# Graph attention on 200,000 edges: twelve chunks of the second superchunk gathered as rows of x, and the first superchunk's edge work placed between its row products

## The chip, the cores and the metric

The kernel runs on one core of a Trainium2 chip. The metric is the device time of one execution in microseconds (us); lower is better. A kernel's time is the median of several executions.

## The reference

A graph with 6250 nodes of 256 features and 200,000 edges, sorted by destination, goes through a layer norm, a ReLU and two graph-attention layers (four heads of 64, then one head of 256), with residuals around them. Cut to what matters:

```python
h = relu(layernorm(x))                      # 6250 x 256
# each layer, on its own input x (h, then the first layer's output):
te = relu(edge_attr @ We + be) * exp(x @ Wo + bo)[src][:, None]   # one row per edge
src2, dst2, ea2 = add_self_loops(src, dst, te, n)   # a loop's attributes: the mean of its node's edges
hx = (x @ Wg).reshape(n, heads, f)
al = leaky_relu(hx.a_s[src2] + hx.a_d[dst2] + (ea2 @ Wge).a_e, 0.2)
m  = segment_max(al, dst2)
al = exp(al - m[dst2]);  al = al / segment_sum(al, dst2)[dst2]
out = segment_sum(hx[src2] * al, dst2) + b
# layer 0: x = relu(out + x)      layer 1: x = out + x, and the first input is added
```

Every edge needs the projected row `hx[src]` of its source node, its logit, the maximum over the edges of its destination, and a weighted sum per destination.

## The kernel before, in words

Edges lie in chunks of 128 (one edge to a partition), and up to C = 24 chunks make a superchunk: 66 superchunks in each layer, 132 steps in all. The instructions of each engine are issued in the order in which they are written; nothing reorders them.

**The prologue** (`prologue`, from L221) makes layer 0's table T, in DRAM: for each node the projected row, its attention terms and the layer-norm pair. The nodes lie in NT = 49 tiles of 128. For a tile, DVE takes the statistics (`stats`, L287), with the Newton steps of the reciprocal root on POOL for the middle groups (L310 to L324); ACT normalises (`norm`, L336); PE transposes twice (`turn`, L342) into a PSUM tile `pT` and ACT copies that back (L344); PE multiplies by the weights in two matmuls, which the trace shows as four (`mult` and `node_rows`, L481) into one of five PSUM tiles `ps`; DVE adds the bias and stores the row in SBUF (`keep` and `node_store`, L485). Tiles go in groups of up to GT = 7; `store` writes a group's rows to T by one DMA from SyncE (L361). Three row tiles `trow` are used in turn.

The 24 chunks of superchunk 0 don't wait for the table: `first_rows` (L276) has POOL gather the rows of x themselves into the gather tile G0, and after the 49 table tiles 24 more row products, through the same five steps, turn them into table rows in place. One loop (L386) is software-pipelined over all 73 tiles; its counter is k, and f = k - NT counts the products after the tables. Between its products the loop calls the other generators: the folds of the attention vectors into the weights (`fold`, L184 to L201, and `fold_e`, L204 to L217; at f = 4, 7 and 12), and one step of the index work per iteration (`indices` and `index_group`, DVE, small operations) once the tables are past. The gathers of x rows are paced by

```python
if k < 9 or k >= 14 and k % 2:
    next(rows0, None)
```

**The edge loop** (`edges`, L693) starts when the prologue is over and its SBUF and PSUM pools are closed. It opens its own: the gather tiles of the second and third superchunk, one-hots, work tiles and three PSUM pools. It then does superchunk 0's first half: `spread` and `parts` (DVE L1113, PE L1228), `blocks`, `rphase1` (PE L1089, ACT L1090), `rphase2` (PE L1098), `adst` (PE L1242), `onehots` (DVE L1207) and `edge_rows` (DVE L1256). Each turn k of the loop does the second half of step k and the first half of step k+1: `gather` of a later step, `logits` (DVE), `ends` (PE L1294), `links` (DVE L1304, L1306, PE L1311), `maxima`, the weighting of the gathered rows (`scale` on DVE, L1378, in layer 0; `scale_rows` on ACT, L1387, in layer 1), `carried` (L1360 to L1368), and the `sums`: 24 matmuls of one-hot by weighted rows (PE L1397), evicted by ACT (L1402).

**Gathers** (`gather`, L989) are POOL's indirect DMAs, one per chunk, from the table. There are three G tiles. The rows of step k+3 go into the tile of step k, each chunk once the sums have read it (`own` in the loop, L746); before the change steps 1 and 2 are gathered in full (24 chunks each) as soon as the table is written, and step 0 not at all, since its rows come from the prologue:

```python
for c in range(0) if st["k"] == 0 and self.CX > last else range(last + 1) if own else (last, *range(last)):
    nc.gpsimd.indirect_dma_start(...)
```

Of the kernel before, what the change touches and what calls it, by code (L numbers as in the profile page):

```python
# [24 lines left out]
I32 = mybir.dt.int32  # L25
# [56 lines left out]
class Kernel:  # L82
# [10 lines left out]
    def run(self):  # L93
# [9 lines left out]
        with ExitStack() as c:  # L103
# [7 lines left out]
            self.prologue()  # L111
# [4 lines left out]
    def consts(self, wp):  # L116
# [104 lines left out]
    def prologue(self):  # L221
# [4 lines left out]
        GT = 7  # L226
        CX = self.CX = min(self.cs[0], NX)
        V = nc.vector
        with ExitStack() as c:
            xp = self.pool("x", 1, c)  # L230
            trows = [xp.tile([P, GT, L.TW], F32, name=f"trow{i}") for i in range(3)]
            wp = self.pool("pw", 2, c)
            pt = self.pool("pt", 2, c, space=PSUM)
# [14 lines left out]
            src0 = wp.tile([P, CX], I32, name="src0", bufs=1)  # L248
            nc.sync.dma_start(src0, a["src"][:, 0:CX])
            load(1)  # L250
            fold, fold_e, edge_weights, more = self.consts(wp)
# [16 lines left out]
            zero = wp.tile([P, L.TW], F32, name="zero", bufs=1)  # L268
            nc.gpsimd.memset(zero, 0.0)
            if NT * P < N + P:  # L270
                nc.sync.dma_start(self.T[0][NT * P:N + P, :], zero[:N + P - NT * P, :L.TW])
            ln = wp.tile([P, NT + CX, 2], F32, name="ln", bufs=1)

            self.G0 = G0 = self.gp[0].tile([P, C, 270], F32, name="G")

            def first_rows():  # L276
# [10 lines left out]
            def stats(*gs):  # L287
# [3 lines left out]
                st = wp.tile([P, w, 6], F32, name=f"st{w}", bufs=2)  # L291
# [45 lines left out]

            def turn(g, i, t):
                pT = pt.tile([P, 2, P], F32, name="pT")
# [6 lines left out]
            def mult(g, i, t):  # L346
                pss[t] = pt.tile([P, 512], F32, name="ps", bufs=5)
                self.node_rows(L, hTs.pop(t), pss[t])

            def keep(g, i, t):  # L350
                row = G0[:, t - NT, :] if g >= g0 else trows[g % 3][:, i, :]
                self.node_store(L, pss.pop(t), row)
                if g >= g0 and i == len(groups[g]) - 1:
                    v = G0[:, t - NT - i:t - NT + 1, L.g:L.g + 1]
                    nc.scalar.activation(v, v, AF.Exp)

            def store(g):
                n, ts, trow = len(groups[g]), groups[g], trows[g % 3]
                nc.scalar.activation(trow[:, :n, L.ln:L.ln + 2], ln[:, ts[0]:ts[0] + n, :], AF.Copy)
                nc.scalar.activation(trow[:, :n, L.g:L.g + 1], trow[:, :n, L.g:L.g + 1], AF.Exp)  # L360
                nc.sync.dma_start(self.T[0][0:NT * P, :].rearrange("(p t) d -> p t d", p=P)[:, ts[0]:ts[0] + n, :],  # L361
# [22 lines left out]
            index = self.indices(wp)  # L384
            kept = 0
            for k in range(-3, len(tiles) + 1):  # L386
                if k == 28:
                    next(index)
                    gi = self.index_load(0, wp)
                    index = chain(index, self.index_group(0, wp, gi))  # L390
                if k > NT + 1:
                    next(index, None)
# [4 lines left out]
                if k == 31:  # L397
                    none = a["x"][N:N + 2 * P, :].rearrange("n d -> (n d)")
# [1369 lines left out]
```

## Time and profile before

| | |
|---|---|
| three runs, us | 4916.92, 4930.53, 4933.85; median 4930.53 |
| the profiled execution, us | 4941.52; its span 4939.7 |
| mean granted TensorE clock | 0.723 |
| PE busy | 2933.2 us, 59% of the span |
| DVE busy | 2452.5 us, 50% |
| ACT busy | 1123.3 us, 23% |
| POOL busy | 2998.2 us, 61% |
| DMA | 592.01 MB, mean 120 GB/s |

The profile is of one execution. Busy time is the time in which an engine executes; PE's weight loads are counted apart (PEld) and overlap with its matmuls. A row of the timeline gives the start (us from the start of the span), the busy time, the engine, line and operation with its operands (out<-in), the number of instructions put together in the row, and in brackets the idle time before it and what ended it; "issue" means that nothing the profile shows was waited for. A group in the table of costliest groups gives busy us, mean ns of one, and idle time before.

### The profile page before, as it was taken

How to read it: one execution, taken by the hardware profiler on the slowest of the kernel's cores; microseconds unless marked ns; L12 is line 12 of the kernel's file. 1: busy time of each engine (PE TensorE's matmuls, PEld its weight loads, DVE VectorE, ACT ScalarE, POOL GpSimd, SP SyncE). 2: the span in 40 equal slices, each digit the busy share in tenths (PEclk: the TensorE clock that was granted, in tenths of full speed). 3: DMA queues.
4: the chain of work that ended last, by engine and by line, in shares of the span. 5: the costliest groups of instructions: out<-in, count | busy, mean ns of one | idle time of the engine just before them, and what ended most of it. 6: DMA issues, size and time to landing. Idle time of an engine off the chain costs nothing.

```text
span 4939.7 us, 37929 instructions
## 1 busy us (share of the span) xinstructions
PE 2933.2 (59%) x10028; PEld 1839.7 (37%) x10028; DVE 2452.5 (50%) x6092; ACT 1123.3 (23%) x2676; POOL 2998.2 (61%) x3217
## 2 busy tenths in 40 slices
PE   7455666666666666666555555656556565655656
PEld 5233333434334343434333333333333333333334
DVE  5366666667666666666644333333333333333335
ACT  4111111111111111111102333323333332333322
POOL 5346666666666666666644666666666666666663
PEclk8677777777777777777777666666666666666667
DMA  6234444444444444444433444444444444443442
GB/s 196 79 98 126 126 135 123 135 129 135 124 129 135 128 128 130 135 121 131 129 109 91 115 114 111 118 112 114 119 113 114 114 120 113 112 120 106 117 118 70
DMA packets 248198, 592.01 MB, mean 120 GB/s; under 512 B 65827, under 2 KB 105209, under 8 KB 247739
## 3 DMA queue, kind: packets, MB, share of 16 engines
q0 software_dynamic: 150048, 422.59, 32.8%
q1 hardware_dynamic: 96957, 164.82, 10.3%
q10 hardware_dynamic: 976, 2.12, 0.1%
q8 instruction: 86, 1.41, 0.1%
q14 instruction: 131, 1.07, 0.1%
HBM read 544.19 MB, written 45.36 MB: 119 GB/s over the span
## 4 chain that ended last, share of the span: by engine, by line
issue 30%; PE 29%; DVE 22%; POOL 10%; another core or an unknown queue 5%; DMA 3%; ACT 1%; DVEq 0%; ACTq 0%
PE u L1397 21%; POOL G L989 10%; DVE G L1378 8%; DMA G<-T,src 3%; PE y L1089 3%; DVE S L1207 2%; PE zad L1098 2%; PE ps L481 1%; DVE m L1326 1%; DVE rt L1256 1%; DVE lb L1113 1%; ACT R L1090 1%; DVE fa L1472 1%; DVE t1row L1562 0%
## 5 line engine op out<-in xcount | busy, mean ns | idle before, releaser
L989 POOL DMA_INDIRECT G<-T,src x3078 | 2934.8, 953 | 1826.8 <-issue 943.2
L1397 PE MATMUL u<-G,S 128*128 128x270 f32 (+1 forms) x6232 | 1873.1, 448 | 1416.3 <-issue 1167.5
L1397 PEld LDWEIGHTS u<-G,S 128*128 128x128 f32 x6232 | 1361.9, 221 | 1860.8 <-issue 1376.8
L1387 ACT ACTIVATE G<-G,kw 128x256 f32<-128x256 f32 x1512 | 609.0, 496 | 0.0
L1304 DVE TENSOR_TENSOR_SCAN cl<-fl,cl,lf 4x129 f32<-4x129 f32 (+1 forms) x130 | 61.1, 470 | 1037.9 <-PE zad L1228 945.9
L1402 ACT ACTIVATE U<-u 128x270 f32<-128x270 f32 (+1 forms) x131 | 51.6, 394 | 2203.3 <-PE u L1397 1642.8
L1378 DVE TENSOR_TENSOR G<-G,kps 128x6144 f32<-128x6144 f32 (+4 forms) x83 | 441.3, 5331 | 0.0
L1207 DVE TENSOR_TENSOR S<-kps,loc 128x3072 f32<-128x3072 f32 x132 | 437.7, 3316 | 4.6
L1089 PE MATMUL y<-ea,webd 64*128 64x256 f32 (+2 forms) x1056 | 358.3, 770 | 45.3 <-ACT R L1090 37.7
L1098 PE MATMUL zad<-R,wea 128*64 128x384 f32 (+1 forms) x1056 | 288.2, 684 | 156.9 <-ACT R L1090 79.1
L1090 ACT ACTIVATE R<-y,webd 128x1024 f32<-128x1024 f32 (+3 forms) x264 | 235.6, 892 | 441.3 <-issue 177.7
L1098 PEld LDWEIGHTS zad<-R,wea 128*64 128x64 f32 x1056 | 83.2, 177 | 395.9 <-issue 247.2
L1429 DVE SCALAR_TENSOR_TENSOR mg<-U,mw 128x1 f32<-128x1 f32 x66 | 14.7, 223 | 347.7 <-ACT mw L1427 176.7
L1089 PEld LDWEIGHTS y<-ea,webd 64*128 64x128 f32 x1056 | 117.0, 271 | 110.6 <-issue 60.4
L1256 DVE STREAM_TRANSPOSE rt<-zad 128x768 f32<-128x768 f32 (+1 forms) x130 | 125.8, 968 | 5.1 <-PE zad L1242 5.1
L481 PE MATMUL ps<-wg,hT 128*128 128x266 f32 x292 | 91.3, 441 | 54.5 <-issue 35.2
L481 PE MATMUL fin<-wg,h1T 128*128 128x260 f32 x264 | 117.1, 588 | 1.6 <-ACT h1T L1489 1.6
L1113 DVE TENSOR_TENSOR lb<-lb,kps 128x1536 bf16<-128x1536 bf16 (+1 forms) x68 | 113.0, 1662 | 0.0
L1360 DVE SCALAR_TENSOR_TENSOR G<-U,kw,G 1x257 f32<-1x257 f32 x62 | 29.5, 475 | 155.9 <-issue 93.1
L1499 ACT ACTIVATE t1row<-t1row 128x1 f32<-128x1 f32 x66 | 13.4, 203 | 368.6 <-DVE t1row L485 160.6
L1311 PE MATMUL lf<-ident,cl 36*128 36x36 f32 (+1 forms) x132 | 37.7, 286 | 94.4 <-issue 60.5
L1294 PE MATMUL lf<-ident,fb 128*36 128x128 f32 (+1 forms) x132 | 52.3, 396 | 57.8 <-DVE fb L1287 45.6
(241 smaller groups left out, 2273.5 us busy)
## 6 DMA issues: line engine op xcount, KB each, us to landing
G<-T,src POOLq DMA_INDIRECT x3078
ea<-in_ea_dram SPq DMA_DIRECT2D x64, 768.0 KB
lb<-locrow SPq DMA_DIRECT2D x64, 384.0 KB
nd<-t1row SPq DMA_DIRECT2D x66, 225.8 KB
tw<-nd SPq DMA_DIRECT2D x66, 225.8 KB
tw<-T SPq DMA_DIRECT2D x66, 117.2 KB
T<-t1row SPq DMA_DIRECT2D x66, 113.8 KB
tw<-in_x_dram SPq DMA_DIRECT2D x66, 112.0 KB
```

The source lines that it names most:

```text
L481: self.nc.tensor.matmul(ps[:, :L.MW], hT[:, k, :], self.wg[L.l][:, k, :], start=(k == 0), stop=(k == 1))
L989: nc.gpsimd.indirect_dma_start(out=G[:, c, 0:L.TW], out_offset=None, in_=st.get("from", self.T[L.l])[0:self.N, :], in_offset=bass.Indirect ...
L1089: nc.tensor.matmul(y[:, i, :n], self.webd[l][r, :], ea[r, w], start=True, stop=True)
L1090: nc.scalar.activation(R[:, :, w], y[:, :, :n], AF.Relu, bias=self.be[l])
L1098: nc.tensor.matmul(st["zad"][i * PH:(i + 1) * PH, o], self.wea[l][0], R[:, i, w], start=True, stop=False)
L1113: V.tensor_tensor(lb[:, :, :n], lb[:, :, :n], self.k_part.unsqueeze(2).to_broadcast([P, i, n]), op=OP.is_equal)
L1207: nc.vector.tensor_tensor(st["S"][:, c0:c1, :], self.k_iota.unsqueeze(1).to_broadcast(w), self.loc[:, o + c0:o + c1].unsqueeze(2).to_broad ...
L1256: V.transpose(rv[:, :32 * c].rearrange("p (b n) -> p b n", b=2), z.rearrange("p (b n) -> p b n", b=2)[:, :, :16 * c])
L1304: V.tensor_tensor_scan(cl[:H, :], fl[:H, :], lf[:H, 0:P + 1], init, op0=OP.add, op1=OP.max)
L1378: nc.vector.tensor_tensor(v, v, pw[:, c0:c1, :].unsqueeze(3) .to_broadcast([P, c1 - c0, H, L.F]), op=OP.mult)
L1387: self.nc.scalar.activation(v, v, AF.Copy, scale=st["w"][:, c:c + 1])
L1397: nc.tensor.matmul(st["u"][:, :L.W], S[:, i, :], G[:, i, 0:L.W], start=(j == 0), stop=(j == c - 1))
```

## The change

**Gathers.** `first_rows` goes on after superchunk 0's 24 chunks and gathers the rows of x of the first CX1 = 12 chunks of superchunk 1, into a one-hot tile that is not yet needed (X). Twelve more tiles join the prologue's loop: 36 row products follow the tables instead of 24, f runs to 35, and the last twelve write into superchunk 1's G tile. `gather` of step 1 then issues 12 gathers from the table instead of 24. The pace of the x gathers changes from every second iteration to every iteration from k = 34 on.

**Pools.** The one-hot, work and index pools are opened at the start. The prologue's x, row and PSUM pools (`early`) are closed at f = 0, right after the last table store; the edge loop's gather and PSUM pools are opened there (`edge_pools`), and the gathers of step 1 (and, as before, of step 2) follow. From then on the row products alternate between two PSUM banks, and the transposes have one, all borrowed from the edge loop's pools (`Banks`, `turned_bank`, `row_bank`). Some scratch tiles share memory with tiles that are used later.

**Table stores.** Rows are stored in groups of GS = 5 tiles (ten stores) rather than in the groups of the loads.

**Order.** `first_edges` runs superchunk 0's edge work between the row products, each piece at a given f, up to the `sums`, whose 24 matmuls go in four pieces at f = 29, 31, 33 and 35. The edge loop leaves out for k = 0 what is done. Index steps start before the tables end (eight in k = 38 to 45) and then go two to an iteration. Folds move from f = 4, 7, 12 to f = 4, 16, 20.

```diff
@@ run
+            self.sp, self.wp, self.xp = (self.pool(n, b, c, side="right") for n, b in (("onehot", 2), ("work", 2), ("index", 1)))
@@ prologue
-        GT = 7
+        GT, GS = 7, 5
         CX = self.CX = min(self.cs[0], NX)
+        CX1 = self.CX1 = min(NX // 2, self.cs[1] - 1) if self.NS > 12 else 0
+        early = ExitStack()
         with ExitStack() as c:
-            xp = self.pool("x", 1, c)
-            trows = [xp.tile([P, GT, L.TW], F32, name=f"trow{i}") for i in range(3)]
-            wp = self.pool("pw", 2, c)
-            pt = self.pool("pt", 2, c, space=PSUM)
+            wp = self.pool("pw", 2, c, side="right")
+            xp = self.pool("x", 1, early)
+            pt = self.pool("pt", 2, early, space=PSUM)
+            trows = [xp.tile([P, GS, L.TW], F32, name=f"trow{i}") for i in range(3)]
...
+            X = self.sp.tile([P, C, P], F32, name="S").rearrange("p (c k) d -> p c (k d)", k=2)
             def first_rows():
...
+                for i in range(CX1):
+                    nc.gpsimd.indirect_dma_start(
+                        out=X[:, i, :], out_offset=None, in_=a["x"][0:N, :],
+                        in_offset=bass.IndirectOffsetOnAxis(ap=src0[:, CX + i:CX + i + 1], axis=0))
+                    yield
...
+            if CX1:
+                xs[len(groups)] = X
+                groups.append(list(range(NT + CX, NT + CX + CX1)))
...
+            def turned_bank(t=0):
+                if t < NT + CX:
+                    q = self.ps_1.tile([P, 512], F32, name="u")[:, 0:2 * P]
+                else:
+                    q = self.ps_1.tile([P, 1024], F32, name="zad")[:, 0:2 * P]
+                return q.rearrange("p (k n) -> p k n", k=2)
+            def row_bank(t=0):
+                banks[0] += 1
+                if banks[0] % 2:
+                    return self.ps_f.tile([P, 512], F32, name="fin")
+                if t < NT + CX:
+                    return self.ps_1.tile([P, 512], F32, name="lf")
+                return self.ps_y.tile([P, 2, 512], F32, name="y")[:, 0, :]
...
-                pT = pt.tile([P, 2, P], F32, name="pT")
+                pT = pt.tile([P, 2, P], F32, name="pT") if t <= NT else turned_bank(t)
...
-                pss[t] = pt.tile([P, 512], F32, name="ps", bufs=5)
+                pss[t] = pt.tile([P, 512], F32, name="ps", bufs=5) if t < NT else row_bank(t)
...
                 if f == 0:
                     keep(*tiles[k - 1])
-                    while kept < g0:
+                    while kept < stores:
                         store(kept)
                         kept += 1
                     self.load_ea(0)
+                    drain(rows0)
+                    early.close()
+                    self.edge_pools(ctx)
+                    self.gather(s0)
+                    self.gather(s1)
+                    pt = Banks()
+                if f in (4, 16, 20):
+                    folds.append(fold(self.L[1], pt) if f == 16 else fold_e(self.L[f // 20], pt))
+                    next(folds[0])
...
-                if k >= NT - 1:
-                    step(g + 2)
+                if NT - 1 <= k < NT:
                     step(g + 2)
                 step(g + 2)
-                if t >= NT:
-                    step(g + 2)
-                if k < 9 or k >= 14 and k % 2:
+                if NT - 11 <= k < NT - 3:
+                    next(index, None)
+                if f >= 0:
+                    next(index, None)
+                    next(index, None)
+                if k < 9 or 14 <= k < 34 and k % 2 or k >= 34:
                     next(rows0, None)
-                if f == 12:
+                if f == 4:
+                    self.nodes(s0)
+                if f == 6:
...
+                self.first_edges(s0, f)
...
+            for q in range(len(tiles) + 1 - NT, 37):
+                self.first_edges(s0, q)
+        self.np_ = self.pool("nodes", 2, ctx, side="right", reuse_waits="tile")
+
+    def first_edges(self, st, f):
+        if f == 11:
+            st["y"] = self.rphase1(st)
+            next(st["y"])
+        if f == 12:
+            self.spread(st)
+            self.parts(st)
+        if f == 14:
+            self.blocks(st)
+            drain(st["y"])
+            self.load_ea(1)
+        if f == 16:
+            self.rphase2(st)
+            self.adst(st)
+        if f == 18:
+            self.edge_rows(st)
+        if 15 <= f < 23 and f % 2:
+            self.onehots(st, 3 * (f - 15), 3 * (f - 13))
+        if f == 24:
+            self.lf = self.ps_1.tile([P, 512], F32, name="lf")
+            self.nc.vector.memset(self.lf[0:4, 0:1], -BIG)
+            drain(self.logits(st))
+        if f == 25:
+            self.ends(st)
+        if f == 26:
+            self.links(st)
+        if f == 27:
+            drain(self.maxima(st))
+        if 28 <= f < 36 and f % 2 == 0:
+            drain(self.scale(st, cuts=(3 * (f - 28), 3 * (f - 26))))
+        if 29 <= f < 37 and f % 2:
+            self.sums(st, (3 * (f - 29), 3 * (f - 27)))
...
+    def edge_pools(self, ctx):
+        self.gp += [self.pool(f"gath{i}", 1, ctx, reuse_waits="tile") for i in range(1, 3)]
+        self.ps_y, self.ps_1, self.ps_f = (self.pool(n, 1, ctx, space=PSUM, reuse_waits="tile") for n in ("ps_y", "ps_1", "ps_f"))
+        self.state = {0: None, 1: None}
...
@@ edges, the loop
-            self.gather(nx)
-            st["rows"] = st["L"].l
-            drain(self.logits(st))
-            self.ends(st)
+            if k:
+                self.gather(nx)
+                st["rows"] = st["L"].l
+                drain(self.logits(st))
+                self.ends(st)
...
@@ gather
-        for c in range(0) if st["k"] == 0 and self.CX > last else range(last + 1) if own else (last, *range(last)):
+        c0 = (self.CX, self.CX1, 0)[min(st["k"], 2)]
+        for c in range(last + 1) if own else (last, *range(c0, last)) if c0 <= last else ():
```

More of the change, by code (lines that the diff above doesn't have):

```diff
@@ L382, in step @@
                         del ahead[q]
-            index = self.indices(wp)
-            kept = 0
+            s0, s1 = self.steps[:2]
+            index = self.indices(wp, drow)
+            kept, stores = 0, -(-NT // GS)
             for k in range(-3, len(tiles) + 1):
+                f = k - NT
                 if k == 28:
                     next(index)
[L389 to L392, printed above, removed]
+                    gi = self.index_load(0, self.xp)
+                    index = chain(index, self.index_group(0, self.xp, gi))
                 if k == 1:
@@ L492, in indices @@
         V = nc.vector
-        sc0 = wp.tile([P, 11, NS], I32, name="sc0", bufs=1)
+        n = 11 * NS
+        t = self.trows1.rearrange("p i w -> p (i w)")
+        assert 2 * n <= t.shape[1] and C * P >= 4 * 32 * C
+        sc0, scf = (x.rearrange("p (k s) -> p k s", s=NS) for x in (t[:, 0:n].bitcast(I32), t[:, n:2 * n]))
         nc.sync.dma_start(sc0, a["sdst"].partition_broadcast(P))
@@ L766, in edges @@
                 self.onehots(st)
-            if st["rows"]:
-                self.scale_rows(st)
-            else:
-                drain(self.scale(st))
-            self.carried(st)
-            self.sums(st)
+            if k:
+                if st["rows"]:
+                    self.scale_rows(st)
+                else:
+                    drain(self.scale(st))
+                self.carried(st)
+                self.sums(st)
             if late:
```

109 lines of the change are left out of this document (47 added, 62 removed).

## The prediction

> **What bounds the kernel now.** I read the page first, for the whole span and its costliest engine.
>
> ```profile
> span 4939.7 us, 37929 instructions
> L989 POOL DMA_INDIRECT G<-T,src x3078 | 2934.8, 953 | 1826.8 <-issue 943.2
> ```
>
> POOL issues 3078 gathers of table rows and is otherwise idle for 1826.8 us, so neither POOL nor any other engine fills the span. 132 superchunks (66 in each of two layers) share the 4939.7 us: 37.4 us each. The change edits only the start, up to the sums of superchunk 0; the loop behind is instruction for instruction as before and hangs on one chain: the gather of superchunk k+3 refills the G tile that the sums of superchunk k free. So the whole span should move by what the start of superchunk 1's sums moves by. That start is the quantity I work out.
>
> Next the timeline of POOL, for the gather runs of the start.
>
> ```profile
> 91.92 1.07 POOL L989 DMA_INDIRECT G<-T,src  x1 [14.90 <-ACT hT L344]
> ...
> 151.58 0.95 POOL L989 DMA_INDIRECT G<-T,src  x1 [0.30 <-issue]
> 210.17 0.95 POOL L989 DMA_INDIRECT G<-T,src  x1 [57.64 <-issue]
> ...
> 238.99 0.95 POOL L989 DMA_INDIRECT G<-T,src  x1 [0.30 <-issue]
> ```
>
> The first run is 48 gathers, those of superchunks 1 and 2, from 91.92 to 152.53, 1.27 us apart (59.66 us over 47 steps). The second, of superchunk 3, waits 57.64 us for the sums of superchunk 0 and ends at 239.94. Now the timeline of PE in the same stretch, and the windows view (length, then busy us and count of PE, PEld, DVE, ACT, POOL, then granted clock, DMA share, GB/s):
>
> ```profile
> 123.68 2.14 PE L481 MATMUL ps<-wg,hT 128*128 128x266 f32 x4 [11.17 <-issue]
> 157.69 2.14 PE L481 MATMUL ps<-wg,hT 128*128 128x266 f32 x4 [12.77 <-ACT hT L344]
> 208.68 11.21 PE L1397 MATMUL u<-G,S 128*128 128x270 f32 x48 [0.95 <-DVE G L1378]
> 242.24 0.32 PE L1311 MATMUL lf<-ident,cl 36*128 36x36 f32 x1 [21.23 <-DVE cl L1306]
> 253.95 11.21 PE L1397 MATMUL u<-G,S 128*128 128x270 f32 x48 [2.16 <-DVE G L1368]
> ```
> ```profile
> 91.90:112.60 20.70, 11.74 (x45) 9.02 (x43) 7.84 (x39) 4.35 (x11) 15.80 (x17) 0.75 0.43 119
> 112.60:157.20 44.60, 5.13 (x12) 3.27 (x12) 1.53 (x5) 1.74 (x4) 30.48 (x32) 0.54 0.41 111
> 219.90:241.20 21.30, 0.91 (x6) 0.40 (x5) 0.20 (x2) 0.57 (x2) 15.17 (x16) 0.62 0.42 109
> 254.90:267.80 12.90, 11.42 (x54) 8.88 (x52) 10.84 (x35) 1.16 (x3) 9.85 (x10) 1.00 0.48 118
> 267.80:287.30 19.50, 0.00 (x0) 0.00 (x0) 0.15 (x1) 0.84 (x3) 13.27 (x14) 0.54 0.42 115
> 300.20:315.20 15.00, 12.96 (x53) 9.99 (x51) 12.67 (x34) 1.12 (x3) 11.36 (x12) 0.89 0.54 148
> 357.50:381.00 23.50, 17.05 (x70) 11.51 (x68) 19.47 (x41) 3.96 (x10) 18.01 (x19) 0.93 0.61 174
> 381.00:390.00 9.00, 1.57 (x3) 0.84 (x4) 0.85 (x6) 0.00 (x0) 4.99 (x6) 0.75 0.46 126
> ```
>
> This is what sets the start. From the first gather of a run PE gets through 45, 54, 53 or 70 matmuls and then nearly stops, with DVE and ACT, until POOL's run ends: 12 matmuls in 44.6 us, 6 in 21.3, none in 19.5, 3 in 9.0. POOL keeps its pace throughout. The profile doesn't say why; I use it as a rule of this kernel, "some 50 matmuls per gather run". Superchunk 0's last row products and all its edge work lie between these stalls, and superchunk 1's sums start at 253.95.
>
> **The change, part by part.** f counts row products after the 49 table tiles. Before, f ends at 23; now it ends at 35.
>
> *Twelve gathers moved ahead.* They leave the first run (48 becomes 36) and join the gathers of x rows, on POOL's queue. There they stand in front of POOL's last block of layer-norm statistics:
>
> ```profile
> 68.45 0.25 POOL L324 TENSOR_SCALAR ln<-sc 128x7 f32<-128x7 f32 x1
> 72.64 0.21 POOL L312 TENSOR_TENSOR sc<-sc 128x13 f32<-128x13 f32 x1 [3.94 <-DVE sc L306]
> ...
> 76.76 0.26 POOL L324 TENSOR_SCALAR ln<-sc 128x13 f32<-128x13 f32 x1
> 77.06 0.60 ACT L336 ACTIVATE h<-x,ln 128x256 f32<-128x256 f32 x1 [1.05 <-POOL ln L324]
> ```
>
> ACT already waits for that block, so there is no slack. By the order of the step calls the block is issued in iteration 37; the new gathers of iterations 27, 29, 31, 33, 34, 35 and 36 precede it. Seven at 1.27 us from 68.70 end at 77.6, the block of 4.38 us at 82.0, not 77.0: 5.0 us late, and tables and first run with it. The tables' last store now holds four tiles, not two: 0 to 2 us, 1 taken. The run starts at 91.9+6.0 = 97.9 and its 36 gathers end at 97.9+45.7 = 143.6. PE came back 5.2 us after the first run (157.69) and 2.3 after the second (242.24); with 3.7, at 147.3.
>
> *How far PE is by then.* Before, it had row product f=10 ahead of it at 157.69; within the run it also folded layer 1's node weights (12 matmuls), which the change puts off. A product is 6 matmuls, two transposes included, so the same allowance reaches f=12.
>
> *From there to the sums.* These rows give the pace:
>
> ```profile
> 162.54 0.64 PE L184 MATMUL pT<-ident,wge 128*128 128x128 f32 x2
> 164.58 0.67 PE L342 MATMUL pT<-ident,h 128*128 128x128 f32 x2
> 165.04 1.98 PE L481 MATMUL ps<-wg,hT 128*128 128x266 f32 x4
> 167.24 1.98 PE L481 MATMUL ps<-wg,hT 128*128 128x266 f32 x4
> 172.15 1.06 PE L481 MATMUL ps<-wg,hT 128*128 128x266 f32 x4
> 173.27 1.06 PE L481 MATMUL ps<-wg,hT 128*128 128x266 f32 x4
> 185.63 0.17 PE L1228 MATMUL zad<-a,Q 128*128 128x12 bf16 x1 [4.80 <-DVE a L1223]
> 185.73 1.23 PE L1089 MATMUL y<-ea,webd 64*128 64x256 f32 x4
> 187.79 2.08 PE L1089 MATMUL y<-ea,webd 64*128 64x512 f32 x4 [0.84 <-ACT R L1090]
> 191.08 2.83 PE L1098 MATMUL zad<-R,wea 128*64 128x384 f32 x8 [1.22 <-ACT R L1090]
> 193.84 0.69 PE L1242 MATMUL zad<-lb,aq 128*128 128x384 bf16 x2
> ```
>
> Sums of superchunk 0 begin at f=29. Seventeen products: three at the 2.20 us seen after a stall, fourteen at 1.12, 22.3. Superchunk 0's own PE work, now between them: 1.23+2.08+2.83+0.69 = 6.8. Folds: the edge one took 2.04 (162.54 to 164.58), the node one has twice the transposes, 6.1 together. PE waiting in line for DVE is new: the edge pieces stand in PE's queue between two products, and the next product, with ACT and the row store behind it, waits. The longest is
>
> ```profile
> 182.78 1.78 DVE L1113 TENSOR_TENSOR lb<-lb,kps 128x1536 bf16<-128x1536 bf16 x1
> ```
>
> and its followers, until the 185.63 above: 2.85. With the waits for logits and links, and two PSUM banks for products where there were five, I take 7 (none at best; 14 if no piece is hidden). In all 42.2: the sums begin at 189.5, not 208.68. Index and one-hot work on DVE costs nothing beside PE as long as DVE keeps up; if not, see the third rival.
>
> *The tail.* The gathers of superchunk 3 start 1.5 us after the sums, at 191.0, and the rule applies again: from f=29 PE has 8 products and 24 sums, 96 matmuls. With 58 done it would stop; 18 gathers are free by then and end at 213.9; 2.3 us later PE runs the other 38 in 8.0: 224.2. Without a stop 8x1.12+11.21 = 20.2 suffice: 209.7. But here POOL in turn pauses whenever PE is late, which no run of before shows, so I take the middle, 217.0. Then superchunk 1 needs, undisturbed, what superchunk 0 needed from 185.63 to 208.68, 23.1: its sums start at 240.1, against 253.95. **Gain 14 us.**
>
> The profiled execution took 4941.52 us, 1.8 more than its span; the three timed runs are 4916.92 to 4933.85, median 4930.53, 11 below it. 4941.5-14 = 4927.5 on the profile's scale, 4916.5 on the median's. A change under 0.3% (14.8 us) can't be told from none here.
>
> [...] First the rows: DVE's longest operation on SBUF tiles beside a run of gathers.
>
> ```profile
> 401.72 6.54 DVE L1378 TENSOR_TENSOR G<-G,kps 128x6144 f32<-128x6144 f32 x1
> 402.58 0.95 POOL L989 DMA_INDIRECT G<-T,src  x1 [0.30 <-issue]
> ...
> 407.58 0.95 POOL L989 DMA_INDIRECT G<-T,src  x1 [0.30 <-issue]
> ```
>
> Five gathers start inside it, 1.25 us apart as ever. [...]
>
> **Rivals.**
> - *PE isn't held any more.* If shorter runs let PE go on: from f=4 at 97.9, 25 products at 1.12 (28.0), 6.8, three folds (8.1), 7, the tail's 20.2 and the chain's 23.1 give 191.1: 63 us earlier, 4868. For it: the runs from 357.5 on stop PE only after 23 us. Against: all runs before that stop it after 10 to 21. A gain of 27 to 63: 0.22.
> - *Nothing is left of it.* Twelve more products (13.4 us), the 5.0 on POOL's queue and both halves of the tail's uncertainty eat the shorter run: full stop in the tail and 14 of in-line waits give 253.95-(224.2+7+23.1) = no gain, 4930. With DVE holding the 36 gathers for the 7.84 us that it was busy in the first window, the forecast's gain is 6 (4924); that alone has 0.04. Together 0.16.
> - *Slower: the two PSUM banks make DVE's queue the clock.* From f=12 on each product must be stored by DVE before the second next can start, and DVE's one-hot, logits, maxima and scaling pieces of 0.8 to 2.9 us stand between the stores. Stores themselves are light:
>
> ```profile
> L485 DVE TENSOR_TENSOR G<-ps,bias 128x266 f32<-128x266 f32 x24 | 10.4, 433 | 68.6 <-remote 28.2 <-issue 16.2 <-PE ps L481 16.0
> ```
>
>   If 1.5 us more per product is lost over the 24 from f=12, 36 us go: 253.95 becomes 276, 22 us slower, 4952. It cancels the gain at 0.6 us per product and counts as slower from 1.2. Against: one store is 0.43 of the 1.12. Chance 0.20.
>
> **How the numbers follow.** The forecast, a gain of 2 to 27 around 14, has 0.42; about half lies beyond 14.8. Faster: 0.22+0.22 = 0.44. Within 0.3%: 0.20+0.15 = 0.35. Slower: 0.21, the third rival and a little of the second. The forecast's own range is 4903 to 4928. Range for 8 in 10: 4884 (half-way into the first rival) to 4950 (most of the third).
>
> **What would show it.** Right: POOL's statistics block about 5 us later, behind x gathers; 36 gathers in the first run, ending near 144; PE nearly idle in its second half; sums of superchunk 0 (L1397's line) near 190 and gathers of superchunk 3 beginning with them; sums of superchunk 1 near 240; the loop unchanged at 37.4 us per superchunk. Wrong: no stall of PE in the first run (first rival); PE waits on row stores spread over f=12 to 35 (third); or a loop whose time per superchunk differs, which none of these cases holds.

## The result

Twenty executions each: 4926.71 us median after (4918.45 to 4941.02), 4933.2 before (4916.92 to 4950.89). The ratio is 0.9985, 95% interval 0.9974 to 0.9996: 7.4 us less (2.0 to 12.8), within the 0.3% taken as no change. The forecast was a gain of 14, to 4916.5, in a range of 4884 to 4950: the time lies in the range, but the gain is about half of the 14, which lies outside the interval.

The profile after, page and timeline of POOL, in the columns of before (L283 and L288 are the gathers of x rows, L322 to L334 the statistics block, L1066 the gathers from the table):

```profile
span 4917.8 us, 38116 instructions
L1066 POOL DMA_INDIRECT G<-T,src x3066 | 2913.0, 950 | 1817.8 <-issue 950.7
```
```profile
67.26 1.08 POOL L288 DMA_INDIRECT S<-in_x_dram,src  x1 [0.17 <-issue]
...
74.89 0.95 POOL L288 DMA_INDIRECT S<-in_x_dram,src  x1 [0.30 <-issue]
...
80.52 0.26 POOL L334 TENSOR_SCALAR ln<-sc 128x13 f32<-128x13 f32 x1
...
96.01 0.94 POOL L1066 DMA_INDIRECT G<-T,src  x1 [8.25 <-ACT hT L382]
...
139.75 0.95 POOL L1066 DMA_INDIRECT G<-T,src  x1 [0.30 <-issue]
189.32 0.95 POOL L1066 DMA_INDIRECT G<-T,src  x1 [48.62 <-issue]
```

Seven gathers of superchunk 1's x rows stand in front of the statistics block, which ends at 80.78, not 77.02. The first run is 36 gathers, from 96.01 to 140.70; then POOL waits 48.62 us for the sums of superchunk 0. PE in the same stretch (L567 is the row product, L1474 the sums):

```profile
109.64 1.06 PE L567 MATMUL fin<-wg,hT 128*128 128x266 f32 x4
...
126.23 1.98 PE L567 MATMUL lf<-wg,hT 128*128 128x266 f32 x4
...
142.39 1.98 PE L567 MATMUL fin<-wg,hT 128*128 128x266 f32 x4
...
148.01 1.98 PE L567 MATMUL lf<-wg,hT 128*128 128x266 f32 x4
...
187.83 3.00 PE L1474 MATMUL u<-G,S 128*128 128x270 f32 x12 [0.49 <-DVE G L1455]
...
209.18 4.19 PE L1474 MATMUL u<-G,S 128*128 128x270 f32 x12
...
241.32 12.89 PE L1474 MATMUL u<-G,S 128*128 128x270 f32 x48 [2.17 <-DVE G L1445]
```

Products come 16 us apart from 109.64 to 142.39, much as before the change (14 to 19 us). Once POOL's run is over they come 1.1 to 2.5 us apart, and up to 4.6 where edge work or folds stand between them. Sums of superchunk 1 start at 241.32 instead of 253.95.

### The profile page after: what moved, and what is told of

Its sections match the earlier page's. It is cut to its first block, busy times and chain, and to the rows that moved or that the text cites. A ratio compares the mean times of both kernels' runs of the same rounds, so it can differ in the third digit from the quotient of the medians.

```text
span 4917.8 us, 38116 instructions
## 1 busy us (share of the span) xinstructions
PE 2927.7 (60%) x10100; PEld 1837.1 (37%) x10100; DVE 2461.0 (50%) x6148; ACT 1132.4 (23%) x2703; POOL 2988.8 (61%) x3216
## 4 chain that ended last, share of the span: by engine, by line
PE 30%; issue 28%; DVE 22%; POOL 10%; another core or an unknown queue 6%; DMA 2%; ACT 2%; DVEq 0%; ACTq 0%; POOLq 0%
PE u L1474 22%; POOL G L1066 10%; DVE G L1455 8%; PE y L1166 3%; DMA G<-T,src 2%; DVE S L1284 2%; PE zad L1175 2%; DVE m L1403 1%; PE ps L567 1%; DVE lb L1190 1%; ACT R L1167 1%; DVE rt L1333 1%; DVE fb L1398 0%; PE zad L1319 0%
## 5 line engine op out<-in xcount | busy, mean ns | idle before, releaser
L1066 POOL DMA_INDIRECT G<-T,src x3066 | 2913.0, 950 | 1817.8 <-issue 950.7
L1474 PE MATMUL u<-G,S 128*128 128x270 f32 (+1 forms) x6232 | 1866.5, 446 | 1421.0 <-issue 1194.1
L1474 PEld LDWEIGHTS u<-G,S 128*128 128x128 f32 x6232 | 1355.1, 220 | 1857.8 <-issue 1392.1
L1455 DVE TENSOR_TENSOR G<-G,kps 128x6144 f32<-128x6144 f32 (+6 forms) x86 | 441.7, 5149 | 0.0
L1284 DVE TENSOR_TENSOR S<-kps,loc 128x3072 f32<-128x3072 f32 (+1 forms) x135 | 438.1, 3245 | 4.7
L567 PE MATMUL fin<-wg,h1T 128*128 128x260 f32 x264 | 116.5, 586 | 1.6 <-ACT h1T L1566 1.6
L1576 ACT ACTIVATE t1rows<-t1rows 128x1 f32<-128x1 f32 x66 | 13.4, 203 | 365.2 <-DVE crow L1443 144.3
L1564 PE MATMUL fin<-ident,fb 128*128 128x128 f32 x132 | 42.7, 379 | 79.9 <-issue 78.3
L1516 ACT ACTIVATE mw<-mw 128x8 f32<-128x8 f32 x66 | 13.8, 209 | 299.9 <-issue 137.9
```

What stands on the lines that cost most here:

```text
L567: self.nc.tensor.matmul(ps[:, :L.MW], hT[:, k, :], self.wg[L.l][:, k, :], start=(k == 0), stop=(k == 1))
L1066: nc.gpsimd.indirect_dma_start(out=G[:, c, 0:L.TW], out_offset=None, in_=st.get("from", self.T[L.l])[0:self.N, :], in_offset=bass.Indirect ...
L1284: nc.vector.tensor_tensor(st["S"][:, c0:c1, :], self.k_iota.unsqueeze(1).to_broadcast(w), self.loc[:, o + c0:o + c1].unsqueeze(2).to_broad ...
L1455: nc.vector.tensor_tensor(v, v, pw[:, c0:c1, :].unsqueeze(3) .to_broadcast([P, c1 - c0, H, L.F]), op=OP.mult)
L1474: nc.tensor.matmul(st["u"][:, :L.W], S[:, i, :], G[:, i, 0:L.W], start=(j == 0), stop=(j == c - 1))
```

## The experiments

What came out first changes how everything else is read. On another chip, **the kernel before took 4002 us, not 4933**, and there the change is slower. The runs met two kinds of chip: the kernel before at 4933 (first comparison), 4874 (pace, half_order, half_rows) and 4937 (split_part); and at 4002 on two chips (all other runs). I call the first kind held, the second free, for what their traces show.

**after_again**, the changed kernel unaltered.

> The changed kernel, unaltered, for a second profile and more times. Its first profile puts the start of superchunk 1's sums at 241.3 us (253.95 before: 12.6 earlier), but the medians of twenty runs each differ by 6.5 us only. Theory A (the start moves the end, one for one): again 238 to 245 us here, and 8 to 14 us below the kernel before. Theory B (the start gains, and the loop behind it gives half back because its stalls fall otherwise): 238 to 245 us here, but the step from superchunk 1 to superchunk 60 takes 5 to 8 us longer than before. Theory C (the start itself varies from execution to execution by about as much as it gained): another start, 5 us or more away from 241.3.

**before_again**, the kernel before unaltered.

> The kernel before, unaltered, for a second profile of it. Theories A and B: sums of superchunk 1 start within 3 us of 253.95; ratio of the times 1.000 within 0.002. Theory C: 5 us or more away from 253.95, since a stall of PE ends with POOL's run or in the middle of it as it happens.

On a free chip: 4014.18 against 4001.95 us, ratio 1.0031 (1.0019 to 1.0043), 12.2 us slower; before_again against its like, 0.9999 (0.9990 to 1.0008). None of theories A to C had this. The kernel before on the free chip (before_again): windows (length, busy us and count of PE, PEld, DVE, ACT, POOL, clock, DMA share, GB/s), then timeline.

```profile
75.30:96.00 20.70, 15.43 (x82) 12.52 (x81) 12.84 (x60) 9.85 (x24) 15.79 (x17) 0.92 0.49 138
96.00:137.40 41.40, 27.80 (x109) 15.14 (x108) 29.63 (x69) 12.29 (x26) 30.46 (x33) 0.75 0.67 175
```
```profile
75.33 1.07 POOL L989 DMA_INDIRECT G<-T,src  x1 [14.95 <-ACT hT L344]
...
137.37 0.94 POOL L989 DMA_INDIRECT G<-T,src  x1 [1.49 <-issue]
```
```profile
135.88 11.21 PE L1397 MATMUL u<-G,S 128*128 128x270 f32 x48 [0.95 <-DVE G L1378]
...
158.30 13.31 PE L1397 MATMUL u<-G,S 128*128 128x270 f32 x48 [4.75 <-DVE G L1368]
```

POOL runs the same gathers at the same 1.25 us each, but PE isn't stopped: 109 matmuls in the last 41.4 us of the run, where on the held chip it did 12 in 44.6 us (112.60 to 157.20). It has done the 24 products and the edge work when POOL's 48th gather is out, and POOL waits 1.49 us. The mean distance between the evictions of two superchunks' sums is 30.2 us (superchunks 16 to 36), which is POOL's 24 x 1.25, against 35.6 on the held chip. So on a free chip POOL's queue sets the end. The changed kernel there:

```profile
81.55 0.94 POOL L1066 DMA_INDIRECT G<-T,src  x1 [10.79 <-ACT hT L382]
...
136.35 0.94 POOL L1066 DMA_INDIRECT G<-T,src  x1 [10.05 <-issue]
...
177.23 0.94 POOL L1066 DMA_INDIRECT G<-T,src  x1 [11.01 <-issue]
```
```profile
134.86 3.00 PE L1474 MATMUL u<-G,S 128*128 128x270 f32 x12 [0.50 <-DVE G L1455]
...
175.74 12.89 PE L1474 MATMUL u<-G,S 128*128 128x270 f32 x48 [2.35 <-DVE G L1445]
```

The account of POOL's queue: it starts 6.2 us later, has 12 gathers less (15.0), and waits 10.05 and 11.01 where it had waited 1.49: 6.2 - 15.0 + 8.6 + 11.0 = 10.8 us slower, 12.2 measured. (It waits once more, 2.62 us before 239.88, which makes it 13.4. In the rows of before_again up to 259.52 POOL waits nowhere else for 1 us or more.) The first wait is for the sums of superchunk 0, which start only 1.0 us earlier than before; the second for those of superchunk 1, 17.4 us later.

**order_alone**, the interleaving without the rows:

```diff
-        CX1 = self.CX1 = min(NX // 2, self.cs[1] - 1) if self.NS > 12 else 0
+        CX1 = self.CX1 = 0
```

> The interleaving alone: no chunk of superchunk 1 is gathered as rows of x (24 row products, 48 gathers in the first run), all else as in the change. Theory 1 (PE is held until the first run ends, and what counts is the run's end plus the work behind it): the run starts near 92, as no x gather stands ahead of the statistics block on POOL, and ends near 152; PE resumes near 157 with about 13 products left instead of 27; sums of superchunk 0 start at 185 to 195, in one piece, and those of superchunk 1 at 225 to 240: as early as the whole change or earlier, 4905 to 4926 us beside 4926.7. Then the twelve gathers moved ahead bring nothing by themselves. Theory 2 (the shorter run is what brings the gain): sums of superchunk 1 at 245 to 254, and less than 4 us gained on the kernel before.

**rows_alone**, the rows without the interleaving (the call of `first_edges` in the loop is dropped, and all its pieces run after it):

```diff
-            for q in range(len(tiles) + 1 - NT, 37):
+            for q in range(37):
```

> The twelve chunks as rows of x alone: superchunk 0's edge work runs after the last row product, not between the products; all else as in the change. Theory 1: PE resumes near 147.5 at the ninth product, the 27 products left and the folds take until about 182, and the edge work up to the sums 27 us, as before (from 181.5 to 208.7): sums of superchunk 0 at 205 to 212, those of superchunk 1 at 240 to 250; 2 to 10 us gained on the kernel before. Theory 2: as much as the whole change, sums of superchunk 1 at 238 to 243. In both, the gap between sums of superchunk 0 and of superchunk 1 goes back to some 45 us or less from the 53.5 of the change, because nothing is put between the sums.

Both on the same free chip, so that the numbers expected for a held PE don't apply. order_alone: 4004.51, ratio 1.0009 (1.0000 to 1.0018). rows_alone: 4028.65, ratio 1.0067 (1.0054 to 1.0081). Their timelines, order_alone and then rows_alone:

```profile
76.58 1.07 POOL L1066 DMA_INDIRECT G<-T,src  x1 [16.29 <-ACT hT L382]
```
```profile
127.52 14.05 PE L1474 MATMUL u<-G,S 128*128 128x270 f32 x48 [3.87 <-issue]
...
165.06 14.07 PE L1474 MATMUL u<-G,S 128*128 128x270 f32 x48 [2.18 <-DVE G L1445]
```
```profile
80.22 0.94 POOL L1065 DMA_INDIRECT G<-T,src  x1 [9.64 <-ACT hT L382]
...
152.36 0.94 POOL L1065 DMA_INDIRECT G<-T,src  x1 [27.38 <-issue]
...
189.80 0.94 POOL L1065 DMA_INDIRECT G<-T,src  x1 [7.71 <-issue]
```

The interleaving does what it says: sums of superchunk 0 at 127.52, 8.4 us earlier than before. But with all of superchunk 0 ahead, superchunk 1's first half no longer runs beside superchunk 0's second: PE begins it at 141.41, behind superchunk 0's sums, where the kernel before began it at 125.86, ahead of them. Superchunk 1's sums come 6.8 us later (165.06 against 158.30) without one more product, and yet the time rises by 2.6 us only. The twelve rows add 10.7 to that (175.74). Without interleaving, POOL waits 27.38 and 7.71: 4.9 - 15.0 + 25.9 + 7.7 = 23.5 us, 26.7 measured. On a free chip the twelve gathers are moved out of a queue whose next work isn't ready; the queue waits instead.

**order_alone_2 and rows_alone_2**, meant for a held chip, met the second free one.

> The interleaving alone (24 row products, 48 gathers in the first run), once more, for a chip where PE is held in gather runs (kernel before at 4870 to 4940 us). Theory H (PE is held from some 14 us after a run's start until 2 to 5 us after its end, and the work behind that sets the start of superchunk 1's sums): PE resumes near 158 to 161 at about the eighth product; sums of superchunk 0 near 200 (some 51 us of work lie behind the run's start on the chip where PE is free, 15 of which fit in ahead of the hold: 160 + 36 = 196), those of superchunk 1 near 250: 4 us gained or nothing. Rival (the interleaving is what gains, the shorter run nothing): as much as the whole change, 238 to 243 for superchunk 1. On a chip where PE is free (4002 us): 4004 as before.

> The twelve chunks as rows of x alone, superchunk 0's edge work behind the last product, once more, for a chip where PE is held. Theory H: PE resumes near 147.5 at the ninth product; on the chip where PE is free the sums of superchunk 0 started 71 us after the run's start, so 147.5 + 71 - 15 = 203 or a little more; those of superchunk 1 at 245 to 255: nothing gained, or up to 8 us. Rival (the shorter run alone brings the gain): 238 to 243 for superchunk 1. On a chip where PE is free: 4028 as before.

4004.56 (ratio 1.0007, 0.9997 to 1.0016) and 4028.6 (1.0064, 1.0050 to 1.0078): the two free chips agree. The two parts alone were not measured on a held chip.

**gate**, on that free chip too:

```diff
         if f == 24:
+            self.nc.gpsimd.tensor_copy(self.gate, self.G0[:, 22, 0:1])
```

> The change with superchunk 2's 24 gathers kept back: POOL first copies one element of the row that product f = 22 stores, so the first run has the 12 gathers of superchunk 1 alone. Theory H on a chip where PE is held: a run of 15 us ends as the hold would begin; f = 9 is reached near 118 instead of 148, the gathers of superchunk 2 run from about 146 to 176, the sums of superchunk 0 start near 158 and are then held; superchunk 1's near 232: up to 9 us less than the change. Rival (PE is slow in this stretch for another reason, its own waits or the index work on DVE): products 7 to 9 stay 16 us apart, and superchunk 0's sums start at 185 to 190 or later. On a chip where PE is free: POOL's queue sets the end and waits about 30 us more for the gate: superchunk 3's gathers start 30 us later, 20 to 30 us slower than the change.

4018.71, ratio 1.0041 (1.0027 to 1.0054): 4.5 us above the change on the other free chip, not 20 to 30.

```profile
80.90 0.95 POOL L1068 DMA_INDIRECT G<-T,src  x1 [10.15 <-DMA flags<-fl]
...
123.44 0.18 POOL L525 COPY gate<-G 128x1 f32<-128x1 f32 x1 [27.78 <-DVE G L573]
```

The expectation added the new wait of 27.78 to the old ones; in fact it took their place: no other of 1 us or more comes after it in the rows up to 258.96. 5.6 - 15.0 + 27.8 - 1.5 = 16.9 us over the kernel before, 16.8 measured: the account holds, my use of it didn't.

**pace**, on a held chip: x gathers of superchunk 1 kept behind the statistics block.

```diff
-                if k < 9 or 14 <= k < 34 and k % 2 or k >= 34:
+                if k < 9 or 14 <= k < 27 and k % 2 or k >= 38:
```

> The change with its twelve gathers of superchunk 1's x rows kept back until POOL's statistics block is issued (from k = 38 on; none in k = 27 to 37). Theory P (where PE is free, POOL's queue sets the end: a gain or loss is what POOL waits more or less, and 1.25 us per gather moved): on a chip where the kernel before takes 4002 us, the first run starts near 76.5 (81.55 in the change) and ends near 121.5; sums of superchunk 0 start 5 us earlier, near 130; POOL still waits some 8 us for them and 11 us for those of superchunk 1; 1.2 - 15.0 + 8 + 11 = 5 us above the kernel before, 4005 to 4009. Rival (superchunk 1's chain of products and edge work sets the end, whatever POOL does): sums of superchunk 1 at 170 instead of 175.7, also 5 to 6 us less than the change; but then POOL's waits sum up to the same 21 us as in the change. On a chip where PE is held (4930 us before): run start 92 to 93, all that follows 4 us earlier than in the change, 4920 to 4926.

4865.96 against 4874.35, ratio 0.9990 (0.9978 to 1.0003). The block ended at 76.0, 4.8 us earlier than in the change, and yet the first run started later, at 98.20:

```profile
76.17 1.07 POOL L288 DMA_INDIRECT S<-in_x_dram,src  x1 [0.15 <-issue]
...
90.74 0.95 POOL L288 DMA_INDIRECT S<-in_x_dram,src  x1 [0.30 <-issue]
98.20 0.95 POOL L1066 DMA_INDIRECT G<-T,src  x1 [6.51 <-ACT h L349]
```
```profile
85.18 1.73 PE L567 MATMUL ps<-wg,hT 128*128 128x266 f32 x4 [2.35 <-issue]
...
90.98 1.17 PE L567 MATMUL ps<-wg,hT 128*128 128x266 f32 x4 [1.61 <-issue]
```

The twelve x gathers in a row are a gather run of their own, and PE's last table products came late in it: 3.63, 1.95 and 3.85 us apart from 81.55 to 90.98, where they had come 1.12 apart. By these rows, what the queue of POOL gave, the hold took; the change itself wasn't run on this chip.

**half_order and half_rows**, same held chip: only superchunk 0's first half goes between the products; its second half runs in the loop as before, with superchunk 1's first half beside it. half_rows has the twelve rows as well, paced as in pace.

```diff
-        if f == 25:
-            self.ends(st)
...
-        if 29 <= f < 37 and f % 2:
-            self.sums(st, (3 * (f - 29), 3 * (f - 27)))
```

> No chunk of superchunk 1 as rows of x, and only the first half of superchunk 0's edge work (spread to edge rows and one-hots) between its row products; its second half (logits to sums) runs in the loop with superchunk 1's first half beside it, as before the change. Theory P, PE free: POOL's first run of 48 gathers ends near 137 as before, sums of superchunk 0 start at 130 to 134 (135.9 before, 127.5 with the interleaving of both halves), those of superchunk 1 at 152 to 156 (158.3 before, 165.1 with both halves): POOL waits nowhere, 4000 to 4004 us, equal to the kernel before within 2 us. Rival (interleaving itself pays on this chip): 3996 or less. PE held: PE resumes near 157 at the eleventh product with superchunk 0's first half hidden behind the rest, sums of both superchunks 6 to 12 us earlier than before, 4921 to 4927 us.

> As the one before, but with the twelve chunks as rows of x (kept back behind the statistics block): superchunk 0's second half follows the 36th product. Theory P, PE free: first run 76.5 to 121.5; last product near 133, sums of superchunk 0 at 144 to 150, so that POOL waits 24 us for them and hardly for superchunk 1's (at 168 to 172): 1.2 - 15.0 + 24 = 10 us above the kernel before, 4010 to 4015. Rival (the second half's pieces between the products are what delays superchunk 1): 4002 to 4006. PE held: sums of superchunk 0 near 200 to 208, those of superchunk 1 at 245 to 252, 4922 to 4930 us.

half_order: 4866.27, ratio 0.9988 (0.9977 to 0.9999). half_rows: 4872.12, ratio 1.0002 (0.9993 to 1.0011). half_order and then half_rows:

```profile
203.81 13.18 PE L1460 MATMUL u<-G,S 128*128 128x270 f32 x48 [1.01 <-DVE G L1441]
...
249.47 14.23 PE L1460 MATMUL u<-G,S 128*128 128x270 f32 x48 [2.17 <-DVE G L1431]
```
```profile
203.79 12.58 PE L1460 MATMUL u<-G,S 128*128 128x270 f32 x48 [1.72 <-DVE G L1441]
...
249.44 11.21 PE L1460 MATMUL u<-G,S 128*128 128x270 f32 x48 [2.17 <-DVE G L1431]
```

Sums of both superchunks start at the same time in the two kernels, 4.9 and 4.5 us earlier than in the kernel before, whose start was seen on the first held chip only; 6 to 12 were expected of half_order. Twelve fewer gathers in the first run and twelve more products come out even. half_order, without any row of superchunk 1, gains 5.8 us (0.5 to 11.2), as much as the whole change gained on the first held chip, within the intervals; the rows add nothing that these runs can see.

**split**, on the second free chip: the kernel before, with a wait for the twelfth gather's landing in every superchunk.

```diff
+            if n == 11:
+                nc.gpsimd.tensor_copy(self.gate, G[:, c, 0:1])
```

> The kernel before, with one wait added in every superchunk: after its twelfth gather POOL copies one element that this gather brings, so POOL pauses until it has landed (some 2.5 us) and each run of 24 falls into two of 12. Theory H in its strong form (a run under about 14 us holds nobody, and a pause of one landing starts the count anew): on a chip where PE is held a step takes 24 x 1.25 + 3 = 33 us instead of 36 to 37: 300 to 450 us less over 130 steps. Weak form (the count goes on through so short a pause): the same time within 20 us, or up to 100 us more. Rival (PE is held by something else than the gathers): every step 3 us longer, 5200 or more. On a chip where PE is free: every step 2.5 to 3 us longer, 4330 to 4400 us against 4002.

4351.45, ratio 1.0874 (1.0857 to 1.0891); steps of 33.15 us (superchunks 16 to 36) instead of 30.20, as expected of POOL's queue.

**split_part**, on another held chip: half_order, with that wait in superchunks 16 to 35 and small POOL fills in 40 to 59.

> The kernel half_order (first half of superchunk 0's edge work between its row products, no chunk of superchunk 1 as rows of x), with two trials in its loop, read from the lengths of the steps: for superchunks 16 to 35 POOL waits for its twelfth gather to land before it goes on, as in split; for superchunks 40 to 59 POOL fills one element of memory after every second gather (some 0.3 us each, so gathers come 1.4 us apart on average). On a chip where PE is held (steps of 35.1 us in half_order): strong form of theory H (a run of 12 holds nobody and a pause of 4 us starts the count anew): steps 16 to 36 at 33 to 34 us; weak form: 35 to 37; held by something else: 38 to 40. For 40 to 60: 34 if the hold comes from the pace of the gathers, 36 to 39 if not. On a chip where PE is free (steps of 30.2): 33.1 for 16 to 36 as in split, 33.5 to 34.5 for 40 to 60 (24 x 1.25 + 12 x 0.3), as POOL's queue sets the step; and the start, which was not seen on such a chip: sums of superchunk 0 at 130 to 134 and of superchunk 1 at 152 to 156, POOL waiting under 2 us for either, against 135.9 and 158.3 before.

Ratio 1.0078 (1.0053 to 1.0103). Steps: 35.67 us undisturbed (6 to 16), 37.73 with the wait (16 to 36), 35.90 with the fills (40 to 60). The wait doesn't shorten the step to the 33 or 34 us of the strong form; it costs 2 us. But it didn't leave POOL with runs of twelve only: POOL goes on from the last twelve gathers of one superchunk straight to the first twelve of the next, so that runs of 24 stand between many of the pauses.

```profile
1005.95 0.94 POOL L1053 DMA_INDIRECT G<-T,src  x1 [11.86 <-PE fin L1555]
...
1024.88 0.29 POOL L1057 COPY gate<-G 128x1 f32<-128x1 f32 x1 [4.23 <-DMA G<-T,src]
...
1057.60 0.18 POOL L1057 COPY gate<-G 128x1 f32<-128x1 f32 x1 [1.93 <-DMA G<-T,src]
```
```profile
1042.75 7.15 PE L1465 MATMUL u<-G,S 128*128 128x270 f32 x26 [0.29 <-DVE G L1436]
1050.38 0.39 PE L1465 MATMUL u<-G,S 128*128 128x270 f32 x1 [0.48 <-issue]
1053.17 0.39 PE L1465 MATMUL u<-G,S 128*128 128x270 f32 x1 [2.40 <-issue]
```

PE worked on for 25 us after the first pause, beside a run of 24 gathers, and then fell to one matmul in 2.8 us. The second pause, of 1.93 us, didn't free it; it stayed slow until POOL's run was over, at 1073 (POOL waits 8.76 us before 1081.77). So this pause of 1.93 us didn't end a hold that had begun. Whether PE stays free when every run has twelve gathers isn't shown.

The fills didn't do what they were meant to. Each took some 0.12 us, inside the 0.30 us that lies between two gathers anyway, and the gathers kept 1.25 us, not 1.4:

```profile
1705.35 0.95 POOL L1053 DMA_INDIRECT G<-T,src  x1 [0.30 <-issue]
1706.30 0.11 POOL L1059 MEMSET gate<- 128x1 f32 x1
1706.60 0.95 POOL L1053 DMA_INDIRECT G<-T,src  x1 [0.19 <-issue]
```

So a slower pace of the gathers was not tested. No version here was shown to beat both kernels on both kinds of chip; half_order wasn't timed on a free one.

## Why the prediction was right, and where not

On the held chip, which it was made from, the steps by their own numbers:

| step | predicted | measured |
|---|---|---|
| statistics block on POOL, later by | 5.0 | 3.8 |
| first run of 36 gathers | 97.9 to 143.6 | 96.01 to 140.70 |
| PE resumes, at product f | 147.3, 12 | about 147.5, 9 |
| from there to the sums of superchunk 0 | 42.2 for 17 products | 40.3 for 21 |
| sums of superchunk 0 start | 189.5 | 187.83 |
| gathers of superchunk 3 start | 191.0 | 189.32 |
| end of the tail | 217.0 (209.7 to 224.2) | 213.37 |
| from there to the sums of superchunk 1 | 23.1 | 27.9 |
| sums of superchunk 1 start | 240.1 | 241.32 |

The start came as forecast: 12.6 us earlier against 13.9, by the mechanism that the prediction gave: PE gets little done in the second half of a shorter first run, takes up work some 10 us earlier than before, and superchunk 0's edge work then runs between the products. That the sum came within 1.2 us is in part luck, as terms that were off made up for each other. Windows of the trace after:

```profile
96.00:112.00 16.00, 7.32 (x26) 5.02 (x23) 9.75 (x56) 2.61 (x6) 12.29 (x13) 0.68 0.83 231
147.30:187.80 40.50, 35.11 (x165) 24.09 (x165) 27.72 (x93) 22.13 (x52) 0.00 (x0) 0.92 0.00 1
```

PE got through 26 matmuls, not "some 50", before the hold: the product count at which it begins is no constant, though its time from the run's start, 14.7 us here, lay among those of before (9.7 to 23.5). So PE came back at f = 9, not 12. The count of products was also off: from f = 12 the sum puts 17 ahead of the sums and 8 behind their start, and the trace has 18 (f = 12 to 29) and 6. The tail behind them was 3.6 us shorter than forecast.

The last term, 23.1 us for superchunk 1 "undisturbed", was 4.8 us too small, because superchunk 1 was disturbed: POOL's gathers of superchunk 3 ran until 221.42, and DVE could start on PE's result only 3.0 us after PE's row for it ends.

```profile
220.12 0.82 PE L1319 MATMUL zad<-lb,aq 128*128 128x384 bf16 x2
223.94 0.98 DVE L1333 STREAM_TRANSPOSE rt<-zad 128x768 f32<-128x768 f32 x1 [5.00 <-remote]
```

Where PE is free the same work takes 23.5 us (order_alone, 141.57 to 165.06), so the term itself was well sized; the hold that it left out is most of the difference.

PE's waits between 147.3 and 187.8 came to 5.4 us (40.50 less 35.11), of the 7 allowed: two PSUM banks didn't make DVE's queue the clock. The longest wait of a product on a row store up to the sums was 0.44 us; behind them there is one of 3.90 us, at 207.25, where DVE itself had stood idle for 5.95 us before it stored PE's product of 197.31. So the third rival is refuted here. DVE holding the gathers for 7.84 us, a term that the second rival took, is shown by no run: the 36 gathers started 1.25 us apart (43.74 us over 35 steps) with the moved DVE work beside them. The row of 6.54 us that the prediction calls DVE's longest on SBUF tiles isn't on such tiles alone: one of its operands, kps, lies in PSUM.

The step that the runs don't bear out is the last, "the whole span should move by what the start of superchunk 1's sums moves by". On the held chip one pair of profiles can't settle it: the two differ by 12.6 us at that mark, by 18.0 at the eviction of the same sums (267.04 against 285.02) and by 21.9 at the end, while the medians differ by 6.5 and two executions of one kernel by up to 34 (4916.92 to 4950.89). Where executions agree within 6.4 us (3997.40 to 4003.83), on the free chip, the mark doesn't set the time. In order_alone it moved by 6.8 and the time by 2.6. In the change it moved by 17.4, superchunk 10's eviction by 10.1 and the last by 11.1: the loop gave part of it back. What share of the 12.6 the held loop gives back isn't settled.

The ground under all of it was the rule that gathers hold PE. On the chip of the profile it held (12 matmuls from 112.00 to 147.30 in the profile after). The prediction took it for a rule of the kernel; it is one of the chip, or of its moment. The first rival, PE not held, was priced at a gain of 27 to 63 us; where PE really isn't held the change loses 12, because there POOL's queue sets the end (10.8 us by its account), which that rival left out. No rival had that mechanism; a slower kernel was forecast with 0.21, but for another reason.

## What to carry to other kernels

Before a stall in one profile becomes the ground of a change, see the kernel on a second chip: the same change gained some 7 us where PE was held and lost 12 where it wasn't. Where one engine's queue sets the end, add up its start, the work taken out and the waits that come in; work moved out of it paid here only as far as the next thing in the queue was ready (rows_alone: 15.0 us of gathers out, 33.6 more of waits in), and a new wait took the place of later ones rather than adding to them (gate: 27.78 us where the change waits 10.05 and 11.01). A superchunk put ahead as a whole lost the overlap with its neighbour (its neighbour's sums came 6.8 us later in order_alone). And look at the rows of a trial before reading its time: here the fills left the pace at 1.25 us, as it was.

## What the hardware showed that was not expected

The same kernel takes 4002 us on two chips and 4874 to 4937 on three sets of runs elsewhere. POOL's gathers keep 1.25 us on both, while PE, on the held ones, gets little done late in a gather run: 12 matmuls in 44.6 us against 109 in 41.4. A pause of 1.93 us didn't end such a hold (split_part, at 1057.60).

The rows say more than "PE is stopped". These stand at the start of the first stall in the kernel before:

```profile
109.67 0.67 PE L342 MATMUL pT<-ident,h 128*128 128x128 f32 x2
110.13 1.98 PE L481 MATMUL ps<-wg,hT 128*128 128x266 f32 x4
```
```profile
123.24 0.39 ACT L344 ACTIVATE hT<-pT 128x256 f32<-128x256 f32 x1 [14.44 <-remote]
134.45 0.43 DVE L485 TENSOR_TENSOR G<-ps,bias 128x266 f32<-128x266 f32 x1 [28.24 <-remote]
```

ACT's copy at 123.24 reads the transposes of 109.67, and DVE's store at 134.45 the product of 110.13. They start 12.9 and 22.3 us after PE's rows end; before the hold it was 0.1 us (ACT's copy at 100.46 behind the transposes of 99.73, DVE's store at 102.25 behind the product of 100.16). The other way nothing is late: PE's next product starts at 123.68, 0.05 us after ACT's copy ends. So in this hold PE's results, or the signals that they were there, reached ACT 12.9 and DVE 22.3 us late, and PE then waited for ACT (11.17 us before 123.68). The ends of matmuls are modelled, so the profile can't tell the two apart. In sums, where the profile shows no wait for another engine between two matmuls, PE's own matmuls came up to 2.8 us apart (split_part, 1050.38 and 1053.17).

What delays PE isn't shown by any run. It wasn't short of instructions: no packet of the instruction queues moved from 107 to 161 us, and PE went on at 157.69. Nor does the granted clock explain it, 0.54 from 112.60 to 157.20: a product took 2.14 us there (123.68) against 1.06 at 172.15, which is far less than the 12.9 and 22.3 us of delay. The number of matmuls and weight loads alone doesn't make a hold either: the free chip shows 109 and 108 of them in 41.4 us (96.00 to 137.40 in before_again) without any. What sets the held chips apart isn't shown.
